# A graph layer with hand-ordered engines: the steps of the first sums end at 2, 5, 8 and 11 tiles, and a block's last join makes its rows later

## The chip, the cores and the metric

The kernel runs on one core of a Trainium2 chip. The metric is device time in microseconds (us) of one execution. TensorE does the matrix products, VectorE (DVE) and ScalarE (ACT) the elementwise work, GpSimd (POOL) issues the indirect DMAs that scatter rows to memory, and SyncE (SP) issues the plain DMAs.

## The reference, cut to what matters

```python
row, col = edge_index                      # 206,250 edges, 6,250 nodes
msg = concat([x[col], edge_attr], axis=1)  # 64 + 64 columns
h = relu(msg @ W1a.T + b1a)                # 128 columns
h = h @ W1b.T + b1b                        # 64 columns
sums = segment_sum(h, row, n_nodes)
counts = segment_sum(ones, row, n_nodes)
agg = sums / maximum(counts, 1)[:, None]
z = relu(concat([x, agg], 1) @ W2a.T + b2a) @ W2b.T + b2b
out = layernorm(x + concat([z, x], 1) @ Wr.T + br)
```

The edges come sorted by one of their two ends (called `dst` in the inputs) and have to be summed by the other.

## The kernel before, in words

The edges are cut into 1,612 tiles of 128 edges, and these into 124 blocks of 13 tiles (`NG`). The nodes are cut into 49 bins of 128. One loop (`for k, ep_ in enumerate(epoch_of)`) runs over the blocks. For a block, TensorE makes the first-layer rows of its edges (`hidden`, L1461), ACT writes them to one of four row buffers (`orow`, L1465; `ROWS = 4`, a block uses buffer k modulo 4), ranks worked out by matrix products with ones (`counts_of`, L1163) give every edge a slot in its bin's part of a table in memory, and POOL scatters the rows to these slots, one indirect DMA for each 128 rows (L1513). `low_bits` (L1452) is ACT's first write to a row buffer in a block. The scatter of block k is issued two blocks later (`LEAD = 2`).

In blocks 2 to 109 some tiles of a block are joined: `join` (L1348) sorts three tiles at a time by node with matrix products against one-hot marks, ACT copies the result to `rj` (L1353), and `join_rows` (L1363, rows written by ACT at L1366) makes the rows of such a join one block later. These rows are scattered in fours, one indirect DMA for each join (`fours`, L1485). A block has 2 joins, or 3 (every second block from 9 to 25, every eighth from 34 to 98). So a block with 2 joins needs 7 + 2 = 9 indirect DMAs, one with 3 joins 4 + 3 = 7, and a block without joins (0, 1, 110 to 123) 13. All together that is 910 + 234.

The table is read back and summed while later blocks are still being made. A step says which tiles of every bin are then surely full: `FULL[0]` lists the ends of the steps for single edges of the first 110 blocks, `FULLQ` those for joined fours. The first four steps of both lists are paired into one stage. A stage opens three blocks (`LATE`) after the block in which both steps are full. `groups_of` cuts a stage into groups of up to three bins (`SUMS`) and 12 tiles (`TILES`), and a written planner deals groups to blocks: per block it adds the stage's remaining tiles divided by the blocks left to the next opening, at most 18 in a block with 2 joins, 10 with 3, 55 with none (`RATES`), and takes groups while this credit is over zero. For each group SP reads its tiles (`read`, L1593), DVE makes one-hot matrices (`nodes_of`, L1627), TensorE multiplies (`summed`, L1647, two records for each tile), and DVE or ACT adds the result to `part` (L1718, L1716). A group dealt to block k is summed in block k + 1. `FULL[1]` and the last stages serve the blocks from 110 on: a stage of 16 groups of 3 tiles, one of 17 groups with 162 tiles that holds the rest of blocks 110 to 121, and 17 groups of 3 tiles for the last two blocks. Behind them the nodes' second layers run group by group.

The order on TensorE, ACT, DVE and SP is that of the program text (`manual_schedule`); POOL's order is left to the compiler. In block k the text goes: `counts_of` for block k + 1, the first parts of `hidden`, the rows of all joins of block k - 1, half of a group's sum (`sum_first`), the ranks of block k + 1's joins (`join_ranks`, L1190), in blocks 4 and 5 some products of weights (L1937 to L1967), the last part of `hidden`, the joins of block k, and the other half of the sum (`sum_rest`). `bins` (L754 to L762) splits the source indices of later blocks into bins; it reads them from the memory that the read buffers `rt` use later.

Of the kernel before, what the change touches and what calls it, by code (L numbers as in the profile page):

```python
# [453 lines left out]
NEAR = 8  # L454
HEAD = 117
NEXT = 468
FULL = ((3, 6, 9, 12), (1,), ())
BIG = 2.0**20
LATE = 3
RD = 6  # L460
# [14 lines left out]
PACED = range(PRE, 123)  # L475
SIDES, ENATS, CHUNK = 2, 2, 2
ON_ACT = 1
FULLQ = (3, 6, 9, 11, 13)
NODES = 8
FIRST = 4  # L480

# [8 lines left out]
def fast_path(  # L490
# [39 lines left out]
    NT = srcT.shape[1]  # L530
# [24 lines left out]
    def joined(k):  # L555
        if not JOIN_FROM <= k < JOIN_TO:
            return 0
        return 3 if k in THRICE else 2
# [7 lines left out]
    def by_bin(of_bin, of_rest):  # L566
        return [of_bin] * (NB - 1) + [of_rest]
# [9 lines left out]
    def low_of(b, n, first=0):  # L577
        _, mean, dev = edges_of(b, n, first)
        return max(0, int(mean - dev)) // P
# [9 lines left out]
    def quads_low(b, n):  # L589
        _, mean, dev = quads_of(b, n)  # L590
        return max(0, int(mean - dev)) * QUAD // P
# [10 lines left out]
    for e, n in enumerate(EPOCHS):  # L602
# [15 lines left out]
        ep_.steps, lo = [], by_bin(0, 0)  # L618
        for t in FULL[e]:
            at = next(k for k in range(n) if low_of(0, k, ep_.first) >= t)  # L620
# [24 lines left out]
    qep.steps, lo = [], by_bin(0, 0)  # L645
    for t in FULLQ:
        at = next(k for k in range(qep.end + 1) if quads_low(0, k) >= t)
# [129 lines left out]
    with (  # L777
# [21 lines left out]
        def mrow_of(k, i):  # L799
            return orows[k % ROWS][:, i * QUAD : (i + 1) * QUAD, :]  # L800
# [230 lines left out]

        NBAD = 15 + 5 * NE + 2 * sum(map(len, FULL)) + 2 * len(FULLQ)
        bad = const.tile([P, NBAD], F32, name="bad")
# [323 lines left out]
        def join_rows(k, i):  # L1357
            _, _, m = made[k]
            rj, mrow = turned.pop((k, i)), mrow_of(k, i)
            for g0 in range(0, QUAD, 2):  # L1360
                ps = hp.take(2, W)
                for j in range(2):
                    done[k, f"join{i}"] = nc.tensor.matmul(  # L1363
                        ps[:, j, :], rj[:, (g0 + j) * P : (g0 + j + 1) * P], m, start=True, stop=True
                    ).ins.name
                nc.scalar.activation(mrow[:, g0 : g0 + 2, :], ps, AF.Relu)  # L1366
                hp.leave(ps)
# [64 lines left out]
        made = {}  # L1432
# [21 lines left out]
        def hidden(k, parts):  # L1454
            rhs, _, m = made[k]
            for k0, n in parts:
                ps = hp.take(SUB, H)
                for j in range(n):
                    c = k0 + j
                    of = c - (BLK - direct(k))  # L1460
                    done[k, c] = nc.tensor.matmul(  # L1461
                        ps[:, j, :], rhs[:WIDE, of * P : (of + 1) * P], m[:WIDE, :H], start=True, stop=True
                    ).ins.name
                phase(k, 4 * H * n, done[k, c])
                nc.scalar.activation(orow_of(k, k0, n)[:, :, :H], ps[:, :n, :], AF.Relu)  # L1465
                hp.leave(ps)
# [254 lines left out]
        def sum_first(k):  # L1721

            if not marked:
                mark()
            g = marked.pop(0)
            halves.append(g)
            g.ps = hp.take(SUMS, H + 1)
            g.half = range(g.b0, g.b0 + -(-g.nb // 2))
            work, done[k, "first"] = summed(g.reads, g.oh, lambda b: g.ps[:, b - g.b0, :], g.half)
            if not joined(k):  # L1730
                phase(k, work, done[k, "first"])
            return g
# [46 lines left out]
        def issue(k):  # L1779

            while to_issue and sum(len(g.reads) for g in issued + marked + halves) + len(to_issue[0]) <= READS:
                issued.append(Sums(k, to_issue.pop(0)))
# [48 lines left out]
        nodes_at = {AHEAD_FROM + EVERY * i: b0 for i, b0 in enumerate(range(0, NB, CHUNK))}  # L1831
        assert JOIN_FROM - 3 < AHEAD_FROM - 1 and max(nodes_at) < JOIN_TO

        bins_at = {NEAR - 2: (HEAD, NEXT), 22: (NEXT, 754), 24: (754, 1040), 26: (1040, 1326), 28: (1326, NT)}
        range_at = {4: (0, ALU.min), 5: (1, ALU.max)}
        assert NEXT % (SEG * BLK) == 0 and NEXT // BLK > max(bins_at) + 3
        for g in range(3):
# [9 lines left out]
        for k, ep_ in enumerate(epoch_of):  # L1847
# [26 lines left out]
            if k > 0:  # L1874
                low_bits(k)
                hidden(k, parts)
            if k > 0 and joined(k - 1):
                for i in range(joined(k - 1)):
                    join_rows(k - 1, i)
                made.pop(k - 1)  # L1880
            if joined(k):
                g = sum_first(k) if due > 0 else None
            if after:
# [35 lines left out]
            if k in range_at:  # L1919
                i, o = range_at[k]  # L1920
# [54 lines left out]
                clear(*clears[k])  # L1975
            issue(k)

            if not joined(k):
                g = sum_first(k) if due > 0 else None
            if after:  # L1980
# [249 lines left out]
```

## Time and profile before

| | us |
|---|---|
| median of 3 runs | 1529.51 (1527.91 to 1533.11) |
| the profiled execution | 1534.22 |
| its span, first to last instruction | 1532.4 |
| TensorE busy | 1440.7 (94%) |
| VectorE busy | 1341.7 (88%) |
| ScalarE busy | 1114.6 (73%) |
| GpSimd busy | 1128.8 (74%) |

Busy time does not count the issue of an instruction or its wait. TensorE's granted clock was 0.983 of its full rate on average over the span.

### The profile page before, as it was taken

The page shows a single profiled execution, that of the slowest core. Times are in us where ns is not written, and L with a number is a line of the kernel's source. Part 1 is how long each engine was busy: PE and PEld are TensorE (multiplying, and loading weights), DVE is VectorE, ACT ScalarE, POOL GpSimd, SP SyncE. Part 2 cuts the span into 40 slices and gives each one's busy share as a digit, 9 for nine tenths or more (in the row PEclk, how much of TensorE's full clock was granted, in tenths as well). Part 3 has the DMA queues.
Part 4 walks back from the last instruction along what each step waited for, and adds up shares of the span by engine and source line. Part 5 has one row for each costly group of instructions (what it writes and reads, how often), then busy time and mean ns, then how long its engine had stood idle before and what let it go on. Part 6 is the DMA issues. An engine that isn't in the chain of part 4 may idle for free.

```text
span 1532.4 us, 33764 instructions
## 1 busy us (share of the span) xinstructions
PE 1440.7 (94%) x11008; PEld 1274.8 (83%) x11008; DVE 1341.7 (88%) x2882; ACT 1114.6 (73%) x2413; POOL 1128.8 (74%) x1198
## 2 busy tenths in 40 slices
PE   5989999987999999999989998999999999999997
PEld 4767777766888988888878888989888899999896
DVE  8789999887898988979889898999999988788787
ACT  3689999996898888878878887887887744332004
POOL 6777777777777777777777777777777777777734
PEclk9899999998999999999999999999999999999999
DMA  8798998967788888777877767777677899999884
GB/s 206 221 301 284 302 303 288 308 188 257 238 262 256 251 253 270 221 229 224 231 238 214 233 213 244 237 227 250 210 242 229 279 322 320 345 343 310 264 275 115
DMA packets 255427, 390.92 MB, mean 255 GB/s; under 512 B 43412, under 2 KB 186838, under 8 KB 255242
## 3 DMA queue, kind: packets, MB, share of 16 engines
q1 hardware_dynamic: 206874, 265.50, 58.7%
q0 software_dynamic: 47840, 122.94, 22.8%
q8 instruction: 90, 1.47, 0.4%
q14 instruction: 95, 0.78, 0.2%
q10 hardware_dynamic: 528, 0.22, 0.1%
HBM read 213.72 MB, written 174.78 MB: 254 GB/s over the span
## 4 chain that ended last, share of the span: by engine, by line
PE 57%; DMA 16%; ACT 11%; DVE 7%; issue 5%; POOL 2%; SPq 1%; DVEq 0%; ACTq 0%; POOLq 0%
PE place L1647 22%; PE place L1348 11%; DMA rows<-orow,rowidx 9%; PE place L1461 9%; PE place L1363 8%; DMA rt<-rows 3%; DMA rows<-orow,qidx 3%; ACT orow L1366 2%; ACT marks L1314 2%; ACT marks L1318 1%; DVE marks L1302 1%; POOL rows L1513 1%; DVE oh L1627 1%; ACT orow L1465 1%; ACT rhs L1414 1%
## 5 line engine op out<-in xcount | busy, mean ns | idle before, releaser
L1513 POOL DMA_INDIRECT rows<-orow,rowidx x910 | 878.3, 965 | 288.0 <-issue 142.5
L1647 PE MATMUL place<-rt,oh 128*128 128x129 f32 x3952 | 483.7, 277 | 15.3 <-ACT orow L1366 5.9
L1647 PEld LDWEIGHTS place<-rt,oh 128*128 128x128 f32 x3952 | 467.7, 193 | 27.2 <-DVE oh L1627 8.3
L1627 DVE TENSOR_TENSOR oh<-ramp,rt 128x768 f32<-128x768 bf16 (+4 forms) x391 | 309.6, 824 | 42.4 <-DMA rt<-rows 41.3
L1465 ACT ACTIVATE orow<-place 128x512 f32<-128x512 f32 (+2 forms) x263 | 142.5, 542 | 224.5 <-PE place L1461 219.3
L1485 POOL DMA_INDIRECT rows<-orow,qidx x234 | 226.1, 966 | 71.3 <-issue 19.8
L1302 DVE TENSOR_TENSOR marks<-quad_ramp,ramp 128x1024 fp32r<-128x1024 f32 x234 | 273.4, 1213 | 1.5 <-ACT z_act L1310 1.5
L1363 PE MATMUL place<-mv,rj 128*128 128x130 f32 x1872 | 242.7, 280 | 33.9 <-ACT orow L1465 20.6
L1348 PE MATMUL place<-marks,side 128*128 128x512 f32 x702 | 267.5, 410 | 0.0
L1461 PE MATMUL place<-mv,rhs 124*128 124x128 f32 x1820 | 262.5, 289 | 4.7 <-ACT orow L1465 3.8
L1363 PEld LDWEIGHTS place<-mv,rj 128*128 128x128 f32 x1872 | 223.1, 192 | 44.5 <-ACT orow L1465 24.5
L1348 PE MATMUL place<-marks,rest 128*64 128x512 f32 x702 | 240.2, 396 | 0.0
L1461 PEld LDWEIGHTS place<-mv,rhs 124*128 124x128 f32 x1820 | 229.6, 197 | 6.2 <-ACT orow L1465 4.0
L1348 PEld LDWEIGHTS place<-marks,side 128*128 128x128 f32 x702 | 134.3, 191 | 51.6 <-issue 2.0
L1366 ACT ACTIVATE orow<-place 128x260 f32<-128x260 f32 x468 | 163.7, 389 | 13.4 <-PE place L1363 4.1
L1314 ACT ACTIVATE marks<-quad_ramp,z_act 128x512 fp32r<-128x512 f32 x234 | 168.9, 722 | 6.1 <-PE place L1348 2.7
L1318 ACT ACTIVATE marks<-marks,ones 128x512 fp32r<-128x512 f32 x234 | 169.8, 725 | 4.1
L1121 DVE TENSOR_TENSOR_SCAN had<-ramp,bins 128x400 bf16<-128x400 bf16 (+2 forms) x124 | 127.2, 1026 | 13.7 <-ACT orow L1452 1.7
L1353 ACT COPY rj<-place 128x512 f32<-128x512 f32 x234 | 133.3, 570 | 1.9 <-PE place L1348 1.9
L1348 PEld LDWEIGHTS place<-marks,rest 128*64 128x64 f32 x702 | 96.0, 137 | 38.6 <-issue 0.8
L1414 ACT ACTIVATE rhs<-rhs,ones 60x896 f32<-60x896 f32 (+2 forms) x116 | 123.7, 1066 | 3.7
L1412 ACT ACTIVATE rhs<-rhs,from_win 60x896 f32<-60x896 bf16 (+2 forms) x116 | 123.6, 1065 | 2.9
(197 smaller groups left out, 1594.7 us busy)
## 6 DMA issues: line engine op xcount, KB each, us to landing
rt<-rows SPq DMA_DIRECT2D x194, 390.0 KB
rt<-rows SPq DMA_DIRECT2D x97, 325.0 KB
rows<-padrow SPq DMA_DIRECT2D x24, 1040.0 KB
rhs<-in_edgeT SPq DMA_DIRECT2D x90, 224.0 KB
enat<-in_edgeJ SPq DMA_DIRECT2D x90, 192.0 KB
rows<-orow,rowidx POOLq DMA_INDIRECT x910
rt<-rows SPq DMA_DIRECT2D x40, 260.0 KB
rt<-rows SPq DMA_DIRECT2D x48, 195.0 KB
```

The lines of the kernel that those rows point to most:

```text
L1302: nc.vector.tensor_tensor(m[:, :n, :], all_q[:, None, :].to_broadcast([P, n, QUAD * P]), z[:, :n, None].to_broadcast([P, n, QUAD * P]), op ...
L1314: nc.scalar.activation(m[:, t, :], all_q, AF.Square, bias=z_acts[k][:, i * JOIN + t : i * JOIN + t + 1], scale=-1.0)
L1318: nc.scalar.activation(m[:, t, :], m[:, t, :], AF.Relu, bias=ones[:, :1], scale=-1.0)
L1348: done[k, f"turn{i}"] = nc.tensor.matmul(ps[: w.shape[1], :], w, m[:, t, :], start=t + p == 0, stop=last and p == 1).ins.name
L1363: done[k, f"join{i}"] = nc.tensor.matmul(ps[:, j, :], rj[:, (g0 + j) * P : (g0 + j + 1) * P], m, start=True, stop=True).ins.name
L1366: nc.scalar.activation(mrow[:, g0 : g0 + 2, :], ps, AF.Relu)
L1461: done[k, c] = nc.tensor.matmul(ps[:, j, :], rhs[:WIDE, of * P : (of + 1) * P], m[:WIDE, :H], start=True, stop=True).ins.name
L1465: nc.scalar.activation(orow_of(k, k0, n)[:, :, :H], ps[:, :n, :], AF.Relu)
L1485: s = nc.gpsimd.indirect_dma_start(out=qep.rows.rearrange("(q r) f -> q (r f)", r=QUAD), out_offset=bass.IndirectOffsetOnAxis(ap=qidx[:, q ...
L1513: s = nc.gpsimd.indirect_dma_start(out=ep_.rows, out_offset=bass.IndirectOffsetOnAxis(ap=rowidx[:, k % RING * BLK + j : k % RING * BLK + j ...
L1627: nc.vector.tensor_tensor(res[:, at_tile : at_tile + nb * n, :], ramp[:, None, :].to_broadcast([P, nb * n, P]), node[:, :, None].to_broadc ...
L1647: m = nc.tensor.matmul(of_bin(b), oh[:, at, :], rows, start=i == 0, stop=i == len(of) - 1)
```

## The change

The first four steps end one tile earlier, so the first stage holds 2 + 2 tiles of a bin in place of 3 + 3, and its groups have three bins in place of two; the tiles that are left go to later stages. The indices of later blocks are split into bins four blocks earlier. The rows of the last join of block k - 1 are made at a later place in block k: behind the first half of the sums, the ranks of the next block's joins and the reads' issue, just ahead of the last part of `hidden`.

```diff
-FULL = ((3, 6, 9, 12), (1,), ())
+FULL = ((2, 5, 8, 11), (1,), ())
...
-FULLQ = (3, 6, 9, 11, 13)
+FULLQ = (2, 5, 8, 11, 13)
...
-        bins_at = {NEAR - 2: (HEAD, NEXT), 22: (NEXT, 754), 24: (754, 1040), 26: (1040, 1326), 28: (1326, NT)}
+        bins_at = {NEAR - 2: (HEAD, NEXT), 18: (NEXT, 754), 20: (754, 1040), 22: (1040, 1326), 24: (1326, NT)}
...
-            if k > 0 and joined(k - 1):
-                for i in range(joined(k - 1)):
-                    join_rows(k - 1, i)
-                made.pop(k - 1)
+            before = joined(k - 1) if k > 0 else 0
+            for i in range(before - 1):
+                join_rows(k - 1, i)
             if joined(k):
                 g = sum_first(k) if due > 0 else None
...
                 clear(*clears[k])
             issue(k)
 
+            if before:
+                join_rows(k - 1, before - 1)
+                made.pop(k - 1)
             if not joined(k):
                 g = sum_first(k) if due > 0 else None
```

## Rows read from the trace of the kernel before

**Rows 1.** The profile's page, its first part: busy time by engine.

```profile
PE 1440.7 (94%) x11008; PEld 1274.8 (83%) x11008; DVE 1341.7 (88%) x2882; ACT 1114.6 (73%) x2413; POOL 1128.8 (74%) x1198
```

**Rows 2.** Groups of instructions by line, POOL: count, busy, mean ns, idle before.

```profile
L1513 POOL DMA_INDIRECT rows<-orow,rowidx x910 | 878.3, 965 | 288.0 <-issue 142.5 <-DMA rows<-orow,rowidx 28.8 <-PE place L1647 17.7
L1485 POOL DMA_INDIRECT rows<-orow,qidx x234 | 226.1, 966 | 71.3 <-issue 19.8 <-ACT orow L1366 12.8 <-DMA rows<-orow,rowidx 10.4
```

**Rows 3.** Timeline of POOL: start, duration, instruction, and idle before it.

```profile
11.08 1.18 POOL L1513 DMA_INDIRECT rows<-orow,rowidx  x1 [6.50 <-DVE rowidx L1269]
...
91.48 0.96 POOL L1513 DMA_INDIRECT rows<-orow,rowidx  x1 [2.54 <-ACT orow L1366]
...
914.31 0.95 POOL L1513 DMA_INDIRECT rows<-orow,rowidx  x1 [0.30 <-PE place L1461]
...
1091.85 0.96 POOL L1513 DMA_INDIRECT rows<-orow,rowidx  x1 [0.30 <-issue]
...
1434.40 0.96 POOL L1513 DMA_INDIRECT rows<-orow,rowidx  x1 [0.30 <-DMA rows<-orow,rowidx]
...
1467.27 0.96 POOL L1513 DMA_INDIRECT rows<-orow,rowidx  x1 [0.30 <-issue]
```

**Rows 4.** Busy time by stretch: length, engines' busy us, PE clock, DMA share.

```profile
290.00:390.90 100.90, 85.53 (x578) 70.47 (x578) 80.64 (x187) 84.40 (x183) 76.68 (x80) 0.95 0.74 235
390.90:895.30 504.40, 486.62 (x3742) 430.88 (x3740) 449.52 (x945) 431.31 (x919) 383.50 (x397) 0.99 0.79 240
...
1220.10:1443.20 223.10, 221.11 (x1928) 216.06 (x1925) 179.28 (x351) 77.16 (x109) 169.15 (x177) 1.00 0.99 317
```

**Rows 5.** Timeline of ACT in block 84: its first write to a row buffer.

```profile
923.20 0.20 ACT L1452 CAST orow<-lo 128x7 f32<-128x7 bf16 x1 [3.80 <-DMA rows<-orow,qidx]
```

**Rows 6.** Timeline of PE: the first product of blocks 85, 86, 87, 111, 112 and 113.

```profile
935.57 0.33 PE L1163 MATMUL cnt_ps<-had,less_ones 128*128 128x400 bf16 x1
...
945.57 0.33 PE L1163 MATMUL cnt_ps<-had,less_ones 128*128 128x400 bf16 x1
...
958.24 0.33 PE L1163 MATMUL cnt_ps<-had,less_ones 128*128 128x400 bf16 x1
...
1229.82 0.31 PE L1163 MATMUL cnt_ps<-had,less_ones 128*128 128x350 bf16 x1
...
1244.49 0.31 PE L1163 MATMUL cnt_ps<-had,less_ones 128*128 128x350 bf16 x1
...
1261.40 0.31 PE L1163 MATMUL cnt_ps<-had,less_ones 128*128 128x350 bf16 x1
```

**Rows 7.** Timeline of PE and DVE around the stage of 162 tiles.

```profile
1421.27 21.88 PE L1647 MATMUL place<-rt,oh 128*128 128x129 f32 x166
1444.86 11.21 PE L1647 MATMUL place<-rt,oh 128*128 128x129 f32 x98 [1.71 <-DVE oh L1627]
...
1421.01 0.95 DVE L1627 TENSOR_TENSOR oh<-ramp,rt 128x768 f32<-128x768 bf16 x1
...
1442.08 0.55 DVE L1718 TENSOR_TENSOR part<-part,place 128x387 f32<-128x387 f32 x1
1443.84 1.42 DVE L1627 TENSOR_TENSOR oh<-ramp,rt 128x768 f32<-128x768 bf16 x2 [1.22 <-DMA rt<-rows]
```

**Rows 8.** Timeline of SP: the first reads of that stage.

```profile
1438.36 1.92 SPq L1593 DMA_DIRECT2D rt<-rows  x4
```

**Rows 9.** Timeline of PE in blocks 4 and 5.

```profile
57.20 1.95 PE L1363 MATMUL place<-mv,rj 128*128 128x130 f32 x16
62.80 0.65 PE L1428 MATMUL place<-w1x_t,rt 65*60 65x128 f32 x2 [3.65 <-DMA rt<-in_xT]
...
82.61 0.45 PE L1964 MATMUL place<-wzz_t,nx 128*65 128x64 f32 x2 [2.96 <-DVE nx L1961]
```

**Rows 10.** Waits of PE for ACT's copy of a join, 100 to 360 us.

```profile
PE place L1363 <- ACT rj L1353: 9.7, 15, 1.7
```

**Rows 11.** Busy time of a stretch of block 4, and PE's granted clock.

```profile
61.20:71.40 10.20, 8.60 (x33) 6.26 (x34) 9.73 (x26) 3.48 (x9) 7.68 (x9) 0.50 0.91 279
```

## Prediction

> **What bounds the kernel now.** The busy times were read first [rows 1]. They point at TensorE, with 94%, and away from POOL, with 74%. The groups by line correct this: POOL's 1,144 indirect DMAs are busy for 878.3 + 226.1 us and have 288.0 + 71.3 us of idle time just before them [rows 2], together 1463.7 us, of which 6.5 us lie ahead of the first one. POOL's timeline goes from 11.08 us to the last issue at 1467.27 us without a hole [rows 3]: one takes about 0.96 us and comes 0.30 us behind the one before, so 1.26 us each. The only wait of size left behind the start of block 4 is 2.54 us at 91.48 us, for the first rows of block 6. From there POOL runs through: a block with 2 joins costs it 9 x 1.26 = 11.4 us, one with 3 joins 8.8 us, one without 16.4 us.
>
> TensorE's own work in a block with 2 joins is less. Blocks 85 and 86 start at 935.57 and 945.57 us and block 87 at 958.24 us [rows 6]; the first summed one group of 12 tiles and the second two, so a block takes 10.0 us with one group, 12.67 us with two, and a tile 0.22 us. With one group a block TensorE is 1.4 us faster than POOL, and POOL holds it back through the row buffers: block 84 may write its buffer only when block 80's scatters have landed. POOL's last issue for block 80 (counted off 9 or 7 to a block) ended at 915.3 us [rows 3], ACT's first write of block 84 came at 923.20 us after a wait of 3.80 us [rows 5], and block 85 began at 935.57 us. Taking off the 12.67 us of work leaves an effective start 7.6 us behind POOL's end. The stretches show the same from outside: from 290.0 to 390.9 us TensorE is busy for only 85.53 of 100.90 us, and from 390.9 to 895.3 us for 486.62 of 504.40 us [rows 4]. Up to block 84 POOL sets the pace.
>
> From 935 us on it is TensorE: it is busy for 221.11 of 223.10 us between 1220.1 and 1443.2 us [rows 4]. The two chains meet again at the stage of 162 tiles. It needs block 121's scatters, whose last issue ends at 1435.4 us [rows 3]; SP issues the first reads at 1438.36 us [rows 8], DVE waits for them until 1443.84 us, and TensorE, which had finished all that came ahead at about 1443.15 us, goes on at 1444.86 us after 1.71 us of waiting [rows 7]. So behind this point lie 1532.4 - 1444.86 = 87.5 us that the change does not touch, and ahead of it TensorE's slack against POOL is 1.7 us. Whatever makes TensorE arrive more than 1.7 us later shows in the time; whatever makes it arrive earlier is lost, unless POOL's chain moves too.
>
> **The change, part by part.** The numbers of tiles come from the planner's formulas, worked out for both lists. The tiles are 1,976 in both, the groups 217 and 209, the reads 391 and 375.
>
> *The steps.* Before, the first stage (25 groups) is dealt to blocks 33 to 57, the second to 58 to 82, the third to 83 to 100 (two groups in every other block); then come 17 groups of 6 tiles up to block 106. Changed, the first stage has 17 groups of three bins, dealt to blocks 24 to 49 with gaps, the second goes to 50 to 74, the third to 75 to 98, and the fourth, 25 groups of 12, to 99 to 111 with two groups in every other block. So sums begin nine blocks earlier, where TensorE idles. But POOL's pace takes this gain away: through block 49 the tiles dealt are 204 before and 194 changed, through block 82 they are 585 and 584. Both kernels stand at the same place by then. Through block 98 they are 861 and 780, and through block 109, the last with joins, 1,036 and 984. TensorE therefore stays in POOL's pace 16 blocks longer and has 52 more tiles to sum behind block 109.
>
> *Where TensorE then stands.* By the same rule as for block 84, block 100 starts effectively 7.6 us behind POOL's end of block 96, which is 1091.85 + 0.96 = 1092.8 us [rows 3]: at 1100.4 us. From there TensorE has work: blocks 100 to 108 are five with two groups and four with one, 5 x 12.67 + 4 x 10.0 = 103.4 us; blocks 109 and 110 with 12 and 24 tiles I estimate from the same price of a tile at 9.4 and 10.6 us. Block 111 starts at 1223.8 us, against 1229.82 us before [rows 6]: 6.0 us earlier. From there blocks 111 and 112 before took 14.67 us with 50 tiles and 16.91 us with 60 [rows 6], 0.224 us a tile, so the 52 tiles cost 11.6 us. The arrival at the stage of 162 tiles becomes 1443.15 - 6.0 + 11.6 = 1448.8 us. The effective start can be 2 us to either side (rows 5 is one case). The 2.0 us for which TensorE was not busy in that last stretch [rows 4] may come again or not: 0 to 2 us less.
>
> *The groups of 6 tiles.* They move from blocks with joins to blocks 111 to 114. DVE takes 0.95 us for the one-hot matrix and 0.55 us for the addition of three bins [rows 7], up to 1.5 us a group, against 6 x 0.224 = 1.34 us on TensorE. Below, they cost nothing, because other groups and the blocks' own products lie between; above, 17 x 0.16 = 2.7 us. I take 1 us.
>
> *The moved rows.* Before, TensorE waits for ACT's copy of a join 15 times, 9.7 us, between 100 and 360 us [rows 10]. The move puts half a sum and the ranks into that wait, and it may remove all of it. But this is in POOL's stretch, so it gives nothing. ACT's writes of these rows and their scatter in fours come some 2 us later; POOL is a block and more behind TensorE and has other scatters to issue. No DMA is added. SP's loads into the edge buffers wait for the last part of `hidden` as before, which lies behind the moved rows.
>
> The start is the exception, because POOL there waits for TensorE. In block 4 TensorE idles 3.65 us for a load, in block 5 2.96 us for DVE [rows 9]. Before, the last join's eight products (half of 16 in 1.95 us, 0.98 us) run ahead of these idles; changed, they run behind them, where the clock is at 0.50 [rows 11] and they may take twice as long, 2 us. In block 5 the DVE chain starts only after block 4's delay. I take 0.9 us from block 4 and 0.6 us from block 5, 1.5 us together, by which block 6's first rows and all of POOL's chain are later. The bounds are 0 (the loads and DVE end last anyway) and 2 x 2 us.
>
> *Bins four blocks earlier* is the same work on DVE and ACT, in POOL's stretch: nothing. The reads of block 24 use memory that the last part of `bins` reads in that same block; one wait of a few us there is covered by the same stretch.
>
> **The sum.** Arrival 1448.8 + 1.0 + 1.5 = 1451.3 us, less about 0.4 us of later waits for reads that are then in time, against 1444.86 us: 6 us more. The profiled span of 1532.4 us (1534.22 us with what lies around it) becomes 1538; the execution profiled was 4.7 us above the median of the runs, so I add the 6 us to the median: 1535.5, say 1535 us. Its own range: 2 to 12 us more, 1531.5 to 1541.5.
>
> **Rivals.** (a) *POOL alone sets the end.* TensorE arrives in time after all: the start of block 100 2 us earlier, no cost of small groups, the 2 us of idle time gone, 1448.8 - 4 = 1444.8 us. Then only the shift of POOL's start counts: 0 to 3 us more, 1529.5 to 1532.5. For it speaks that the two chains meet so closely; against it, the 52 tiles. 27%.
>
> (b) *TensorE is the bound throughout* and the earlier sums fill its idle time. Of the 15.4 us not busy between 290.0 and 390.9 us, plus 17.8 us up to 895.3 us [rows 4], the first 15 us would come off: 1514 us. It decides if POOL's 1.26 us are no limit but a wait that shrinks when TensorE is earlier. Against it speaks that the intervals are the same in blocks of every kind. The Trainium skill, "Perfetto Trace Analysis", Identifying the Most-Contended Engine, takes the occupancy of GpSimd as a fair measure of how close that engine is to its limit, and the most occupied engine as the one to improve; by its rule POOL has a quarter of its time free, and filling TensorE's gaps pays these 15 us. This trace disagrees: POOL's 74% goes with no gap over 0.31 us in long stretches. 6%.
>
> (c) *More is lost.* The start loses its 4 us and more stretches at half clock, or the reads of blocks 99 to 111, which come just after their scatters have landed, keep TensorE waiting where it has no slack left: 12 to 25 us more, about 1546. The DMA share of 0.99 from 1220 to 1443 us [rows 4] speaks for it; that the tiles summed in a us stay the same speaks against. 11%.
>
> My forecast has the remaining 56%.
>
> **How the numbers follow.** The runs of before lie 0.34% apart, so 0.3%, 4.6 us, is about what a measurement tells from no change. Of the forecast some 70% lies above 4.6 us, 39%; with all of (c) and little of (a) slower is 0.52. Most of (a) and the rest of the forecast are the same, 0.41. Faster is (b) and a little noise, 0.07. The range leaves out (b) and half of (c): 1527.5 to 1545.
>
> **What would show it.** Right: POOL's last issue 1 to 3 us later, with intervals still of 1.26 us; block 111 starting near 1224 us; the stage of 162 tiles starting near 1451 us with no wait of DVE for its reads; L1363 waiting less for `rj`. Wrong: a start of that stage at 1445 to 1447 us behind a wait (rival a), holes in POOL's timeline, or POOL's chain ending earlier than 1467 us.

## The result, and the profile after

The changed kernel takes 1551.57 us in the median of 5 runs (1549.47 to 1555.06), the kernel before 1529.51 us in as many (1527.91 to 1533.11): a ratio of 1.0137, 95% interval 1.0122 to 1.0153, 22 us more. The forecast was 1535 us. Its profiled execution took 1551.57 us with a span of 1549.7 us, 17.3 us over the span of before, whose profiled execution lies 4.7 us above its median. In thirteen of the eighteen later runs the engines wait longer for each other and the kernel before takes 1,906 to 1,928 us (on one chip before and after a run at the usual time), so these stand apart below, and of their times only ratios are used.

The busy time hardly moved, so the 17 us are no work. The page of the changed kernel, its first part and the groups by line (answers to [rows 1, 2]):

```profile
PE 1441.8 (93%) x11008; PEld 1276.0 (82%) x11008; DVE 1339.8 (86%) x2866; ACT 1114.0 (72%) x2405; POOL 1129.4 (73%) x1198
...
L1513 POOL DMA_INDIRECT rows<-orow,rowidx x910 | 879.2, 966 | 286.7 <-issue 141.5
...
L1485 POOL DMA_INDIRECT rows<-orow,qidx x234 | 225.7, 964 | 85.1 <-issue 25.5
...
L1366 ACT ACTIVATE orow<-place 128x260 f32<-128x260 f32 x468 | 165.3, 386 | 70.8 <-PE place L1363 65.0
```

One number stands out: the idle time ahead of POOL's scatters in fours, L1485, is 85.1 us instead of 71.3 us [rows 2], and beside it is ACT's L1366, which writes the rows of a join and waits 65.0 us for TensorE's L1363. Most of that wait is no loss: with the rows moved alone (below) it is 55.9 us, and the time grows by 0.2%. POOL's timeline shows that this is no drift but single holes (start, duration, instruction, idle before it and what ended it; answers to [rows 3]):

```profile
289.79 0.96 POOL L1513 DMA_INDIRECT rows<-orow,rowidx  x1 [1.25 <-DMA rows<-orow,rowidx]
...
303.41 0.95 POOL L1485 DMA_INDIRECT rows<-orow,qidx  x1 [3.84 <-ACT orow L1366]
...
334.75 0.96 POOL L1485 DMA_INDIRECT rows<-orow,qidx  x1 [8.84 <-ACT orow L1366]
...
1480.37 0.96 POOL L1513 DMA_INDIRECT rows<-orow,rowidx  x1 [0.30 <-issue]
```

Two waits of 3.84 and 8.84 us, where 0.30 us is the rule, and the last issue 13.1 us later (1480.37 against 1467.27 us). What POOL waited for is found by following the names back through the block in which the longer hole arises, block 28, which TensorE starts at 314.21 us. SP's queue, DVE, PE and ACT there:

```profile
308.45 7.79 SPq L1573 DMA_DIRECT2D rows<-padrow  x7
316.29 2.70 SPq L1593 DMA_DIRECT2D rt<-rows  x2
```

```profile
324.19 0.96 DVE L1627 TENSOR_TENSOR oh<-ramp,rt 128x768 f32<-128x768 bf16 x1 [7.72 <-DMA rt<-rows]
327.26 0.96 DVE L1627 TENSOR_TENSOR oh<-ramp,rt 128x768 f32<-128x768 bf16 x1 [2.12 <-DMA rt<-rows]
```

```profile
325.20 1.23 PE L1647 MATMUL place<-rt,oh 128*128 128x129 f32 x4 [7.92 <-DVE oh L1627]
328.28 2.95 PE L1647 MATMUL place<-rt,oh 128*128 128x129 f32 x12 [1.85 <-DVE oh L1627]
...
332.94 1.11 PE L1363 MATMUL place<-mv,rj 128*128 128x130 f32 x8
```

```profile
333.64 0.83 ACT L1366 ACTIVATE orow<-place 128x260 f32<-128x260 f32 x2 [12.99 <-PE place L1363]
```

Read from below: POOL's scatter in fours at 334.75 us needs ACT's L1366 at 333.64 us; this needs the eight products of L1363 at 332.94 us, the moved rows; they now stand behind half of a sum and the ranks; the sum waited 7.92 and 1.85 us for its one-hot matrix; DVE waited 7.72 and 2.12 us for the reads; and SP issued these reads at 316.29 us, right behind seven clears of the table (L1573) that held its queue from 308.45 us for 7.79 us. The first stage of sums now opens in block 24, but the clears of the first table run up to block 27, and within a block the clear stands ahead of the reads. Before, the sums begin in block 33, past these clears.

The waits cost TensorE more than their length. Block 28 lasts 24.0 us; in the kernel of "reads first" below, where its sum does not wait, it lasts 12.24 us. Of the 11.8 us between, 9.8 us are the two waits. Most of the rest is slower work, 13.93 us busy against 11.67 us: right behind the wait of 7.92 us the granted clock is 0.50, the lower of TensorE's two levels (1.2 of 2.4 GHz). The stretch from 325.20 to 331.00 us in the changed kernel, then block 28 in reads first (length, engines' busy us, PE clock, DMA share):

```profile
325.20:331.00 5.80, 3.95 (x16) 3.61 (x17) 3.60 (x8) 0.00 (x0) 0.71 (x1) 0.50 0.98 303
```

```profile
308.85:321.09 12.24, 11.67 (x86) 9.99 (x86) 10.86 (x31) 10.79 (x23) 9.50 (x10) 1.00 1.08 349
```

POOL never gets this back: its 241st indirect DMA, behind the longer hole, comes 13.8 us later than in the kernel before, and its last, the 1,144th, 13.1 us later. The stage of 162 tiles starts at 1462.52 us instead of 1444.86 us [rows 7], and behind it lie 87.2 us as before. Block 111 starts at 1234.43 us, 4.6 us later than before [rows 6], where 6.0 us earlier was forecast. PE in the changed kernel:

```profile
1234.43 0.31 PE L1163 MATMUL cnt_ps<-had,less_ones 128*128 128x350 bf16 x1
...
1462.52 11.21 PE L1647 MATMUL place<-rt,oh 128*128 128x129 f32 x98 [0.39 <-DVE oh L1627]
```

### The profile page after: what moved, and what is told of

Its sections match the earlier page's. It is cut to its first block, busy times and chain, and to the rows that moved or that the text cites. A ratio compares the mean times of both kernels' runs of the same rounds, so it can differ in the third digit from the quotient of the medians.

```text
span 1549.7 us, 33691 instructions
## 1 busy us (share of the span) xinstructions
PE 1441.8 (93%) x11008; PEld 1276.0 (82%) x11008; DVE 1339.8 (86%) x2866; ACT 1114.0 (72%) x2405; POOL 1129.4 (73%) x1198
## 4 chain that ended last, share of the span: by engine, by line
PE 49%; DMA 18%; DVE 12%; ACT 10%; issue 6%; POOL 3%; SPq 2%; DVEq 0%; POOLq 0%; ACTq 0%
PE place L1647 19%; PE place L1348 9%; DMA rows<-orow,rowidx 8%; PE place L1461 7%; PE place L1363 7%; DMA rt<-rows 5%; DVE marks L1302 4%; DVE oh L1627 3%; DMA rows<-orow,qidx 3%; POOL rows L1513 2%; ACT orow L1366 2%; ACT rhs L1414 2%; ACT orow L1465 2%; ACT rhs L1412 1%; ACT marks L1318 1%
## 5 line engine op out<-in xcount | busy, mean ns | idle before, releaser
L1513 POOL DMA_INDIRECT rows<-orow,rowidx x910 | 879.2, 966 | 286.7 <-issue 141.5
L1363 PE MATMUL place<-mv,rj 128*128 128x130 f32 x1872 | 263.8, 285 | 31.7 <-ACT orow L1465 18.1
L1485 POOL DMA_INDIRECT rows<-orow,qidx x234 | 225.7, 964 | 85.1 <-issue 25.5
L1348 PE MATMUL place<-marks,side 128*128 128x512 f32 x702 | 266.8, 409 | 1.2 <-DVE nx L1821 1.1
L1363 PEld LDWEIGHTS place<-mv,rj 128*128 128x128 f32 x1872 | 231.9, 194 | 38.1 <-ACT orow L1465 20.2
L1461 PE MATMUL place<-mv,rhs 124*128 124x128 f32 x1820 | 253.5, 283 | 0.8 <-DVE rhs L1420 0.8
L1348 PE MATMUL place<-marks,rest 128*64 128x512 f32 x702 | 239.1, 395 | 0.0
L1461 PEld LDWEIGHTS place<-mv,rhs 124*128 124x128 f32 x1820 | 229.5, 197 | 2.0 <-DVE rhs L1420 1.1
L1366 ACT ACTIVATE orow<-place 128x260 f32<-128x260 f32 x468 | 165.3, 386 | 70.8 <-PE place L1363 65.0
L1348 PEld LDWEIGHTS place<-marks,side 128*128 128x128 f32 x702 | 133.8, 191 | 53.5 <-DVE nx L1821 2.2
L1348 PEld LDWEIGHTS place<-marks,rest 128*64 128x64 f32 x702 | 95.4, 136 | 38.4 <-issue 0.4
```

Of the source, the lines that this page charges most:

```text
L1348: done[k, f"turn{i}"] = nc.tensor.matmul(ps[: w.shape[1], :], w, m[:, t, :], start=t + p == 0, stop=last and p == 1).ins.name
L1363: done[k, f"join{i}"] = nc.tensor.matmul(ps[:, j, :], rj[:, (g0 + j) * P : (g0 + j + 1) * P], m, start=True, stop=True).ins.name
L1461: done[k, c] = nc.tensor.matmul(ps[:, j, :], rhs[:WIDE, of * P : (of + 1) * P], m[:WIDE, :H], start=True, stop=True).ins.name
L1485: s = nc.gpsimd.indirect_dma_start(out=qep.rows.rearrange("(q r) f -> q (r f)", r=QUAD), out_offset=bass.IndirectOffsetOnAxis(ap=qidx[:, q ...
L1513: s = nc.gpsimd.indirect_dma_start(out=ep_.rows, out_offset=bass.IndirectOffsetOnAxis(ap=rowidx[:, k % RING * BLK + j : k % RING * BLK + j ...
```

## The experiments

**The change once more.** The kernel as it is, run beside the others.

> The changed kernel as it is, on the chip of these experiments. In the five experiments so far the kernel before took 1,906 to 1,928 us instead of 1,530 us, TensorE's signals come later there, and POOL has idle time in nearly every block. Theory A (there the moved rows cost by delaying ACT's queue in every block, and the steps cost nothing): the same ratio to before as with reads first or an opening at block 29, 1.010 to 1.014. Theory B (the clears and late reads of blocks 24 to 28 cost there too): 1.017 or more, above those two.

It came out at 1550.84 us beside 1531.39 us, a ratio of 1.0120 (1.0084 to 1.0156), with the kernel before at its usual time, so that its two theories, which are about late signals, were not tested. Its profile, of the longest of its four executions (1554.52 us), has the same holes, 3.98 us at 303.80 us and 11.87 us at 338.11 us. The next four kernels were run together, beside a kernel before of 1531.13 us.

**Rows ahead.** Is it the moved rows that starve POOL?

```diff
+            if k > 0 and joined(k - 1):
+                for i in range(joined(k - 1)):
+                    join_rows(k - 1, i)
+                made.pop(k - 1)
-            before = joined(k - 1) if k > 0 else 0
-            for i in range(before - 1):
-                join_rows(k - 1, i)
...
-            if before:
-                join_rows(k - 1, before - 1)
-                made.pop(k - 1)
```

> The changed kernel with the rows of a block's last join back at their old place, ahead of the sums; steps and bins stay changed. Theory (the late rows starve POOL: the scatter of the last four waits until the first half of a sum whose reads are late has gone through TensorE): the holes of 3.84 and 8.84 us in POOL's blocks 25 and 27 go or shrink to under 5 us together, POOL's last issue comes back from 1480.4 us to 1468-1472 us, and the time to 1533-1540 us. Rival (late reads alone cost it: TensorE's blocks 26 and 28 last 19 and 24 us wherever the rows stand, and POOL starves a block later): holes of over 8 us in all, in blocks 26 to 29, and 1545-1552 us.

1544.06 us, 1.0085 (1.0054 to 1.0116): between the two ranges. The holes sum to over 8 us, as the rival has it, but they stand in POOL's blocks 25 and 27, as in the changed kernel, and not a block later. POOL, SP and PE in this kernel:

```profile
300.46 0.96 POOL L1513 DMA_INDIRECT rows<-orow,rowidx  x1 [1.92 <-PE place L1461]
...
331.07 0.95 POOL L1513 DMA_INDIRECT rows<-orow,rowidx  x1 [8.15 <-PE place L1461]
...
1476.20 0.96 POOL L1513 DMA_INDIRECT rows<-orow,rowidx  x1 [0.30 <-issue]
```

```profile
304.73 7.96 SPq L1573 DMA_DIRECT2D rows<-padrow  x7
312.74 2.65 SPq L1593 DMA_DIRECT2D rt<-rows  x2
```

```profile
322.19 1.20 PE L1647 MATMUL place<-rt,oh 128*128 128x129 f32 x4 [5.77 <-DVE oh L1627]
...
329.91 0.89 PE L1461 MATMUL place<-mv,rhs 124*128 124x128 f32 x6
```

The join's fours now go out in time, and POOL stops at the very next scatter, until the last part of `hidden` is done (L1461, 329.91 to 330.80 us), which has stood behind the same half of the sum all along. That scatter's own rows are not what is missing: they are rows of block 27, which ACT wrote by 312.1 us. It waits by a rule of the kernel that the words on the kernel before do not mention (a cut, with `j` the tile of the block):

```python
{6: 9, 8: BLK - 1, 10: "turn1", 12: "rest"} if j0 == 2 * JOIN      # pace, L1507
...
done.get((k + 1, pace.get(j))) if joined(k)                       # L1532
```

In a block k with 2 joins the scatter of tile 8 waits for the product of the last tile of block k + 1, the scatter of tile 10 for a join of that block, and that of tile 12 for the second half of its sum; with 3 joins tiles 10 to 12 wait in the same way. So a late sum stops POOL even where it has rows. Block 27 had five scatters left, 5 x 1.26 = 6.3 us by my estimate, that could have gone into the hole of 8.15 us; no run leaves the rule out.

So the theory of the late rows fell: two holes of 10.1 us together are left of 12.7 us (15.9 us in the second profile of the change). The late sum is the cause, the rows only widen the hole.

**Reads first.** SP issues a block's reads ahead of its clear.

```diff
-            if k in clears:
-                clear(*clears[k])
             issue(k)
+            if k in clears:
+                clear(*clears[k])
```

> The changed kernel with the reads of a block issued on SP ahead of the block's clear of the table instead of behind it. Theory (the reads of blocks 25 and 27 land late because 1.04 MB clears stand ahead of them in SP's queue): these reads land 2 us earlier in block 25 and 5-8 us earlier in block 27, TensorE's wait in block 28 falls from 7.9 us to under 3 us, POOL's holes sum to under 4 us instead of 13, time 1534-1540 us. Rival (the reads are late because their scatters or buffers are, or because the DMA engines are full of clears anyway): same holes, 1548-1553 us.

1540.90 us, 1.0059 (1.0041 to 1.0078). SP and POOL:

```profile
302.68 1.19 SPq L1593 DMA_DIRECT2D rt<-rows  x2
303.91 9.87 SPq L1573 DMA_DIRECT2D rows<-padrow  x7
```

```profile
335.58 0.96 POOL L1485 DMA_INDIRECT rows<-orow,qidx  x1 [0.56 <-ACT orow L1366]
...
1471.77 0.96 POOL L1513 DMA_INDIRECT rows<-orow,rowidx  x1 [0.30 <-issue]
```

The holes are gone; the longest between 290 and 345 us is 0.56 us. Two lines in other order give back half of the loss. The time lies just above the theory's 1540 us, and the wait for reads goes on to the next sum, 6.90 us on DVE and 4.54 us on TensorE at 328.13 us, but there what POOL has in hand lasts just long enough. Whether the reads were late because the clears' issue held SP's queue or because the clears' data were moved first is not told apart; the new order changes both.

**Opening at block 29.** The first stage is dealt from block 29 on, behind the last clear of the first table.

```diff
         open_at = [min(max(st.at for st in stage) + LATE, NGR) for stage in summing]
+        open_at[0] = 29
```

> The changed kernel with the first stage dealt from block 29 on instead of from block 24, behind the last clear of the first table (block 27); steps, bins and moved rows stay. Theory: no hole in POOL's blocks 24 to 28; block 111 starts near 1221-1225 us, the stage of 162 tiles near 1449-1451 us, time 1533-1538 us, which is what the prediction gave. Rival (what costs is more tiles behind block 109, or the moved rows in POOL's stretch): 1545 us or more although POOL has no hole there.

1537.82 us, 1.0043 (1.0020 to 1.0066), as the theory had it, and no hole in blocks 24 to 28. The profiled execution was the longest of its seven (1542.22 us); in it block 111 starts at 1229.84 us and the stage of 162 tiles at 1453.66 us, both later than the theory's. Its timeline shows where most of that comes from: in block 4 TensorE waits twice as long for a load as in [rows 9], and from block 6 on POOL's chain is 5.1 us late. PE and POOL:

```profile
65.81 0.68 PE L1428 MATMUL place<-w1x_t,rt 65*60 65x128 f32 x2 [7.72 <-DMA rt<-in_xT]
```

```profile
1474.65 0.96 POOL L1513 DMA_INDIRECT rows<-orow,rowidx  x1 [0.31 <-issue]
```

**Rows alone.** The kernel before with the moved rows, and its own steps and bins: the diff of rows ahead, turned round.

> The kernel before with the rows of a block's last join moved behind half of the sums and the ranks; old steps and bins. Theory (the move does harm only where a sum's reads are late while POOL has no rows in hand): the first sums fall in blocks 34 and 35, where TensorE waits 0.85 and 4.02 us before, so at most one hole of 0-4 us there and otherwise a chain of 1.26 us; time 1527-1534 us. Rival (the moved rows cost by themselves, in every block, as they did by 1.9% on the chips where all signals came late): POOL's chain ends over 8 us later and the time is 1540 us or more.

1533.69 us, 1.0021 (1.0008 to 1.0035). No hole anywhere behind block 5. The profiled execution was the longest of its ten (1537.86 us). POOL and PE:

```profile
1469.59 0.96 POOL L1513 DMA_INDIRECT rows<-orow,rowidx  x1 [0.30 <-issue]
```

```profile
1445.70 24.53 PE L1647 MATMUL place<-rt,oh 128*128 128x129 f32 x190 [3.68 <-DVE oh L1627]
```

POOL's last issue is 2.3 us later, all of it from the start (block 4 waits 6.09 us there), and TensorE waits for POOL's rows at the stage of 162 tiles, as in the kernel before.

**Where all signals are late.** The last four kernels, and two more, also ran where the kernel before takes 1,906 to 1,928 us. All expectations here were written for 1,530 us, so these runs do not decide them. The two more are rows ahead together with reads first, and the kernel before with three more blocks of 3 joins, which takes six indirect DMAs off POOL:

```diff
-THRICE = (*range(9, 27, 2), *range(34, 99, 8))
+THRICE = (*range(9, 33, 2), *range(34, 99, 8))
```

Rows ahead and reads first together was expected, in two runs:

> The changed steps and bins with both repairs: the reads of a block ahead of its clear, and the last join's rows at their old place ahead of the sums. Theory (what is left is the 52 tiles behind block 109, which make TensorE arrive at the stage of 162 tiles at 1448.8 us plus whatever POOL is late at block 96, against 1444.86 us before): holes under 2 us, 1533-1537 us beside 1,530 us, a ratio of 1.002 to 1.0045. Rival (the late rows were not what kept reads first at 1541 us): 1538-1542 us.

> The changed steps and bins with both repairs: the reads of a block ahead of its clear, and the last join's rows at their old place ahead of the sums. Theory (what is left is the 52 tiles behind block 109, which make TensorE arrive at the stage of 162 tiles at 1448.8 us plus whatever POOL is late at block 96, against 1444.86 us before): holes under 2 us, 1533-1537 us beside 1,530 us, a ratio of 1.002 to 1.0045. Rival (the late rows were not what kept reads first at 1541 us): 1538-1542 us.

Three more joins:

> The kernel before with three more blocks of 3 joins (27, 29 and 31), which replaces nine of POOL's scatters of single tiles by three scatters in fours: six indirect DMAs fewer, 7.6 us of POOL's chain at 1.26 us each, in the stretch from 290 to 360 us where TensorE idles for 10 us. Theory (POOL's chain sets the pace up to block 84 and carries TensorE's start with it): POOL's last issue 7 us earlier, the stage of 162 tiles starting near 1438-1440 us, time 1523-1526 us, a ratio of 0.995 to 0.997. Rival (TensorE's work bounds the kernel and the three joins add to it): 1531-1538 us.

> The kernel before with three more blocks of 3 joins (27, 29 and 31), which replaces nine of POOL's scatters of single tiles by three scatters in fours: six indirect DMAs fewer, 7.6 us of POOL's chain at 1.26 us each, in the stretch from 290 to 360 us where TensorE idles for 10 us. Theory (POOL's chain sets the pace up to block 84 and carries TensorE's start with it): POOL's last issue 7 us earlier, the stage of 162 tiles starting near 1438-1440 us, time 1523-1526 us, a ratio of 0.995 to 0.997. Rival (TensorE's work bounds the kernel and the three joins add to it): 1531-1538 us.

Rows ahead was expected, in the order of its three runs:

> The changed kernel with the rows of a block's last join back at their old place, ahead of the sums; steps and bins stay changed. Theory (the late rows starve POOL: the scatter of the last four waits until the first half of a sum whose reads are late has gone through TensorE): the holes of 3.84 and 8.84 us in POOL's blocks 25 and 27 go or shrink to under 5 us together, POOL's last issue comes back from 1480.4 us to 1468-1472 us, and the time to 1533-1540 us. Rival (late reads alone cost it: TensorE's blocks 26 and 28 last 19 and 24 us wherever the rows stand, and POOL starves a block later): holes of over 8 us in all, in blocks 26 to 29, and 1545-1552 us.

> The changed kernel with the rows of a block's last join back at their old place, ahead of the sums; steps and bins stay changed. On a chip where the kernel before takes about 1,530 us, theory (the late rows starve POOL behind a sum whose reads are late): holes in POOL's blocks 24 to 28 under 5 us together, time 1533-1540 us. Rival (late reads alone cost it): over 8 us of holes, 1545-1552 us.

> The changed kernel with the rows of a block's last join back at their old place, ahead of the sums; steps and bins stay changed. Theory (the late rows starve POOL behind a sum whose reads are late): holes in POOL's blocks 24 to 28 under 5 us together, time 1533-1540 us beside a kernel before of about 1,530 us. Rival (late reads alone cost it): over 8 us of holes, 1545-1552 us.

Rows alone:

> The kernel before with the rows of a block's last join moved behind half of the sums and the ranks; old steps and bins. Theory (the move does harm only where a sum's reads are late while POOL has no rows in hand): the first sums fall in blocks 34 and 35, where TensorE waits 0.85 and 4.02 us before, so at most one hole of 0-4 us there and otherwise a chain of 1.26 us; the start of the chain is 0-1 us earlier as in the changed kernel; time 1527-1534 us. Rival (the moved rows cost by themselves, in every block): POOL's chain ends over 8 us later and the time is 1540 us or more.

> The kernel before with the rows of a block's last join moved behind half of the sums and the ranks; old steps and bins. On a chip where the kernel before takes about 1,530 us, theory (the move does harm only where a sum's reads are late): one hole of POOL of 0-4 us about blocks 33 to 35, time 1527-1534 us. Rival (the moved rows cost by themselves, in every block, as they did where all engines were held up between their instructions): 1540 us or more.

Reads first:

> The changed kernel with the reads of a block issued on SP ahead of the block's clear of the table instead of behind it. Theory (the reads of blocks 25 and 27 land late because 1.04 MB clears stand ahead of them in SP's queue): these reads land 2 us earlier in block 25 and 5-8 us earlier in block 27, TensorE's wait in block 28 falls from 7.9 us to under 3 us, POOL's holes sum to under 4 us instead of 13, time 1534-1540 us. Rival (the reads are late because their scatters or buffers are, or because the DMA engines are full of clears anyway): same holes, 1548-1553 us.

> The changed kernel with the reads of a block issued on SP ahead of the block's clear of the table. On a chip where the kernel before takes about 1,530 us, theory (the reads of blocks 25 and 27 are late because clears of 1.04 MB stand ahead of them in SP's queue): POOL's holes sum to under 4 us, time 1534-1540 us. Rival (the DMA engines are full of clears anyway, or the reads wait for something else): same holes, 1548-1553 us.

Opening at block 29:

> The changed kernel with the first stage dealt from block 29 on instead of from block 24, behind the last clear of the first table (block 27); steps, bins and moved rows stay. Theory: no hole in POOL's blocks 24 to 28; block 111 starts near 1221-1225 us, the stage of 162 tiles near 1449-1451 us, time 1533-1538 us, which is what the prediction gave with no start-up loss. Rival (what costs is more tiles behind block 109, or the moved rows in POOL's stretch): 1545 us or more although POOL has no hole there.

> The changed kernel with the first stage dealt from block 29 on, behind the last clear of the first table (block 27); steps, bins and moved rows stay. On a chip where the kernel before takes about 1,530 us, theory: no hole in POOL's blocks 24 to 28, block 111 near 1221-1225 us, the stage of 162 tiles near 1449-1451 us, time 1533-1538 us. Rival (the tiles behind block 109 or the moved rows cost the rest): 1545 us or more although POOL has no hole there.

What was measured, twice each:

| kernel | ratio to before, 95% interval | again |
|---|---|---|
| rows ahead | 0.9997 (0.9973 to 1.0022) | 0.9976 (0.9962 to 0.9991) |
| rows alone | 1.0186 (1.0140 to 1.0233) | 1.0192 (1.0161 to 1.0224) |
| reads first | 1.0124 (1.0080 to 1.0168) | 1.0115 (1.0080 to 1.0150) |
| opening at block 29 | 1.0118 (1.0076 to 1.0160) | 1.0118 (1.0085 to 1.0150) |
| rows ahead and reads first | 0.9958 (0.9932 to 0.9983) | 0.9966 (0.9946 to 0.9985) |
| three more joins | 0.9974 (0.9953 to 0.9995) | 1.0019 (0.9998 to 1.0041) |

A single further run of rows ahead took 1920.99 us beside 1927.87 us. In these runs the moved rows cost 1.9% by themselves and the new steps nothing. POOL has idle time in nearly every block (587.1 us ahead of L1513 in rows ahead, against 288.0 us [rows 2]), so that a single hole may not count, while an order that makes engines wait for each other once more does; that this is the reason is argued, not shown. TensorE's waits from 400 to 1500 us, in the second runs of rows alone and then rows ahead:

```profile
PE place L1348 <- ACT orow L1366: 52.4, 33, 3.6
```

```profile
PE place L1348 <- ACT orow L1366: 3.4, 3, 1.5
```

The next join (L1348) waits for ACT's L1366, which comes later with the rows moved. Rows ahead and reads first together, the new steps with both troubles taken away, is the one version that was faster than the kernel before in both its runs, by 0.3 to 0.4%; the changed kernel itself was not measured there. Three more joins came out on both sides of 1. For the last two kernels the questions stay open: what the steps cost without either trouble at 1,530 us, and whether fewer scatters shorten the kernel there, was not measured.

## Why the prediction was wrong

**What bounds the kernel** held. POOL's chain of 1.26 us sets the pace and carries its delay to the end, and TensorE comes to bind behind it. (The reading of POOL's timeline before passes over two shorter waits behind the start of block 4, 1.51 us at 77.63 us and 1.05 us at 262.53 us; no term of the sum rests on them.) This can be put in one line: the forecast had TensorE arrive at the stage of 162 tiles at 1448.8 us if POOL is not late. Adding what POOL's last issue is late by gives the measured start of that stage in every kernel with the new steps:

| kernel | POOL's last issue, us | later than 1467.27 | 1448.8 + that | stage starts |
|---|---|---|---|---|
| changed | 1480.37 | 13.1 | 1461.9 | 1462.52 |
| changed, again | 1484.30 | 17.0 | 1465.8 | 1466.06 |
| rows ahead | 1476.20 | 8.9 | 1457.7 | 1456.15 |
| reads first | 1471.77 | 4.5 | 1453.3 | 1452.72 |
| opening at block 29 | 1474.65 | 7.4 | 1456.2 | 1453.66 |

So the sum of the planner's arithmetic, the price of a tile and the start of block 100 behind POOL's end of block 96 was right within 2.6 us. In reads first, block 111 starts at 1228.11 us; without POOL's 4.5 us that is 1223.6 us, where 1223.8 us was forecast.

**The step that failed** is the one that gave the earlier sums and the earlier bins nothing because they fall into POOL's stretch: "one wait of a few us there is covered by the same stretch". The sums were counted as TensorE's work and as tiles, and not as reads in SP's queue. That queue holds the clears up to block 27, and nothing in the part on the steps looks at them. The waits that came of it were not a few us but 7.92 + 1.85 us in block 28 and 2.45 + 1.38 us in block 26 (the profile puts the 2.45 us down to ACT's `rhs`; in reads first they are gone), and the half clock behind them made the blocks longer still, 24.0 and 18.7 us. The cover was thin: after TensorE's start of block 26 POOL goes on for 11.3 us, after that of block 28 for 11.7 us, about one block of scatters, and then stops. It can't turn to others: the scatters behind come in a fixed order, and the kernel's `pace` ties them to TensorE's next block, which the prediction does not mention either. What was named as work behind other work has a limit, and the sum had no term for passing it. The 13.1 us by which POOL is late stand where the forecast had 1.5 us; with them the forecast's own terms give 1448.8 + 13.1 = 1461.9 us.

**The moved rows** gave nothing and cost about what was said: 2.6 us between the medians, 3.2 us by the ratio of rows alone, against 1.5 us with bounds of 0 and 4. "POOL is a block and more behind TensorE" was true behind block 5 in that kernel. Whether they cost more together with late reads is not clear: the ratio of rows ahead is 0.35% below that of the changed kernel run again, but the two intervals overlap; the holes go from 12.7 and 15.9 us to 10.1 us. The wait for ACT's copy between 100 and 360 us was expected to shrink and didn't: 10.7 us in 11 waits, against 9.7 us in 15 [rows 10].

**The start** was 0.7 us earlier in the changed kernel, not 1.5 us later: the same issue of POOL, counted from the first, comes at 93.31 us instead of 94.01 us. But the wait in block 4 that sets it is not a constant. It took 3.65 us before [rows 9], 3.77 and 4.51 us in the two profiles of the changed kernel, 3.05 us with the rows ahead, 0.74 us with reads first (with 3.32 us for DVE just behind), 6.09 us with the rows alone and 7.72 us with the opening at block 29. In the five profiles with moved rows that issue of POOL comes 0.7 us earlier to 5.1 us later than before, 1.6 us later on average. That is near the 1.5 us of the forecast, but one profile of each doesn't tell how much of it is the kernel and how much the execution.

**The rivals.** Rival (c) had the size, about 1546 us, and a cause of the right kind, late reads that keep TensorE waiting, but in blocks 99 to 111, where the DMA share is 0.99, and there TensorE had no wait for reads until block 118 (2.26 us). Rival (b) is refuted: in reads first the sums begin early, no hole over 1.0 us is left behind block 5, and POOL's issues still come every 1.26 us; the time is 9.8 us above the kernel before, not 15 us below. Rival (a) did not come either: TensorE reaches the stage of 162 tiles after a wait of only 0.39 us, so it was late itself. Of the signs named, "holes in POOL's timeline" was the one that appeared.

**What the steps cost without the trouble.** Reads first and the opening at block 29 are the change as the prediction imagined it, and they came out 9.8 and 6.7 us above the kernel before, where 6 us was forecast. In the first, POOL's last issue is 4.5 us late: 0.8 us from the start, and much of the rest from holes of 0.6 to 1.0 us in blocks 18, 22, 28, 34 and 67. That what is left is the 52 tiles rests on the table above; no run at 1,530 us tries the steps alone.

## What to carry to other kernels

When work is moved earlier into a stretch where its engine idles, list its transfers too, and what already stands in the queue that will issue them: here 7.8 us of clears stood ahead of a sum's reads, and an engine that had time to spare took the chain that had none down with it. Cover has a size; compare the wait not with the idle time of the engine that waits but with the work that the bound engine has in hand (here one block, 11.3 and 11.7 us), and look for rules in the kernel that tie that work to the engine that waits. And where parts of a change are judged, try them apart: the moved rows alone cost 0.2%, the whole change with its reads in time 0.4 to 0.6%, with late reads 1.2 to 1.4%.

## What the runs showed of the hardware

Rows ahead has profiles from both kinds of run, at 1,544 us and where all signals are late, on the same chip. DVE, ACT and POOL are busy for as long in both (1347.3, 1107.6 and 1127.8 us late, 1339.2, 1111.6 and 1128.8 us at 1,544 us), and yet the late span is 24% longer. TensorE is busy for 1592.1 us instead of 1445.6 us, at a mean granted clock of 0.921 instead of 0.975; the rest of the 367 us is time in which it waits. One case: DVE's L1214 waits for TensorE's counts. In the kernel before it starts 0.30 us after DVE fell idle, released by the last product of the counts (L1202); in rows ahead, late, it starts 3.03 us after, when joins queued behind the counts are also done:

```profile
758.22 0.48 DVE L1214 TENSOR_REDUCE ramp<-cnt_ps 128x6 f32<-128x300 f32 x1 [0.30 <-PE cnt_ps L1202]
```

```profile
975.46 0.48 DVE L1214 TENSOR_REDUCE ramp<-cnt_ps 128x6 f32<-128x300 f32 x1 [3.03 <-PE place L1348]
```

What delays the signals, the profiles don't show. The moved rows, which cost 0.2% at 1,530 us, cost 1.9% there.
